# Adding each head's relu to the sum by a DMA, with the half-step lists laid out anew: a two-layer graph kernel on one core

## The chip, the cores and the metric

The kernel runs on one core of one Trainium2 chip. The metric is the device time of one execution in microseconds, median of several runs; lower is better. The engines are named as the profile names them: PE (TensorE, matmuls; PEld is its weight load), DVE (VectorE), ACT (ScalarE), POOL (GpSimd) and SP (SyncE, which issues most DMAs). POOL can issue DMAs too, and an adding DMA (`accum_op=ALU.add`), which adds what it reads to what stands at its destination, is issued there.

## The reference

There are 16 images (graphs) with N = 1024 nodes of D = 128 features, and an adjacency matrix of 0 and 1 for each image.

```
# layer 0: attention over the graph, with three gates
h  = x @ Ww.T + Wb
e  = (h @ A) @ h.T ;  e = e + e.T
s  = where(adj > 0, e, 0)
att = softmax(s, axis=1) * adj
hp = relu(att @ h)
ic, fc, oc = sigmoid(hp @ wi_u + x @ wi_x), sigmoid(... wf ...), sigmoid(... wo ...)
x  = layernorm(x + oc * tanh(ic * hp + fc * x))
# layer 1: four heads
for each head:  h = x @ conv_w + conv_b
                sc = (h @ attn_w) @ h.T
                hh = relu(tanh(adj * sc) @ h)
x  = layernorm(x + relu(relu(mean of hh over the heads) + x))
```

## The kernel before

**Images and steps.** The main loop runs over the 16 images. In the turn of image b, PE computes layer 1 of image b, while pieces of layer 0 of image b+1 (and the first ones of image b+2) and the end of layer 1 of image b-1 are strewn in between. A turn has 32 steps: step = head * 8 + m. Each step has two half steps (q = 0, 1), so a turn has 64 of them. They are called slots here, 0 to 63.

**The lists.** Which piece runs in which slot is written out by hand, in three lists of 64 strings: `FIRST` for image 0, `PLAN` for images 1 to 14, `LAST` for image 15. `slot(n)` goes through the names of string n and emits their instructions. Each engine works its instructions in the order in which they are emitted, so a list decides every engine's order. The names:

- `d5`, `m5`: `differ` and `differ_more` of pair 5 (below). If the pair's scores come later in the turn than the slot, the pair of the previous image is meant (`m15`, and `d14`, `d15` at the end for this image).
- `e`: the next piece of `layer1_end` of the previous image: first the DVE transpose of the sum of heads (`turn_sums`, L335), which goes by way of DRAM to `y`; then two elementwise operations (L1040, L1042) that read `y`, a layernorm in parts, and the DMA to the output (L1046, issued on POOL).
- `r`, `j`, `u`: weights of layer 1. `rows` are projections, `join_rows` four small POOL operations on `hx` and `h` for a group of one head (L796 to L799), `head_uT` a PE projection that ACT copies (L283).
- Capital letters and the rest: pieces of layer 0 of the next image, such as `S` (scores, read by ACT), `T` (transposes), `E` (edges, L475 on POOL), `A` (mask and exponentials), `B` (weighing and the matmuls of the attention), `H` and `h` (the projection `h` and its bias, L411 on DVE), `Q` (projection of q), `G`, `R` (second half of the attention), `P Y F f i o I O V N D` (gates, tanh, layernorm, transposes). With a `+` ahead the piece belongs to the image after the next.

**Pairs.** In layer 1 a head has eight blocks of 128 rows, taken two by two, block i and block i + 4. Such a pair (class `Pair`, number 4 * head + i, so 16 per image) takes two steps, four slots. In each slot PE computes 128 x 512 scores (tag `sc`, three PSUM buffers), DVE multiplies them with the adjacency (L829, L831), and after two slots ACT takes the tanh (L836). The second product, tanh times h, is done with seven products instead of eight, as in Strassen's way: `differ` is a DVE addition (L840), `differ_more` a DVE addition and an adding DMA of 256 KB on POOL's queue (L891, L892). The early products (`early`, numbers 1, 2, 3) of pair p run in slots 4p+4 and 4p+5, the late ones (`late`, numbers 4 to 7) in slots 4p+10 and 4p+11; the late ones read what the adding DMA wrote.

**The end of a head.** After its last pair the products are put together: `keep_early` on ACT, `combine` on DVE (L924 to L929), `sum_up` (L936 on POOL, then the relu on ACT, L940 for head 0, straight into the sum, or L942 for the others) and half a step later `sum_end`, which adds the relu `w` (128 x 1024) to `sum_t` (L948, on POOL). For heads 1 and 2 this falls into the same turn, for head 3 into the next one: `sum_up` after slot 8, `sum_end` after the even slot 10 and ahead of the odd slot 11. There `turn_sums` can begin. In image 15, head 3 is done in another way (`last_step`, `last_back`), and `ready_last` transposes the sum of heads 0 to 2 on PE (L1000), right after the last `sum_end`. So `sum_end` adds 3 x 16 - 1 = 47 times.

**Other order.** `land()` in each step issues the waiting second halves of transposes through DRAM on SP. `w` has one buffer, pairs have three.

Of the kernel before, what the change touches and what calls it, by code (L numbers as in the profile page):

```python
# [15 lines left out]
ALU = mybir.AluOpType  # L16
# [3 lines left out]
P = 128  # L20
# [4 lines left out]
def two_layer_adjacency_kernel(  # L25
# [19 lines left out]
    nc = tc.nc  # L45
    B, N, D = x.shape
# [761 lines left out]
    acc1_t, sum_t, kept, hx_t = {}, {}, [], {}  # L808
# [4 lines left out]
    class Pair:  # L813
# [130 lines left out]
        def sum_end(self):  # L944
            if self.i < BH - 1 or self.hd == 0:
                return
            w = acc1_t[self.b, self.hd, 1][:, :4].rearrange("p k n -> p (k n)")
            nc.gpsimd.tensor_add(sum_t[self.b], sum_t[self.b], w)  # L948

    def last_step(b, m):  # L950
        hd = H - 1
# [171 lines left out]
    for g in range(2):  # L1123
# [2 lines left out]


    PLAN = [
        "B3", "E4 L5 T5 m15", "", "j0.0 A4 L6", "", "d0", "E5 T6 m0", "E6 r2 r3 B4",
        "d1 L7 r6 A5 r7", "m1", "B5 j0.1", "A6 d2", "+W E7", "", "u1.0 e", "+Q0 u1.1 m2 B6 A7",  # L1130
        "B7 j1.1 j1.0", "d3", "+L0 m3 e X R0 e", "+E0 G0 G1 G2 e e e G3 G4 G5",
        "G6 G7 e +L1 R1 d4", "P e m4", "", "", "", "+L2", "+E1 d5", "m5 d6 u2.0 e", "+H0 Y +h0",
        "+Q1 m6 F +S0", "+T0", "+H1 u2.1 +A0 +h1 j2.0", "d7 +S1 f i +T1", "", "m7", "o d8 +S2",
        "j2.1", "+S3 u3.0 +T2 m8 I0", "I1", "", "", "d9 O0 +S4", "m9 O1", "Va", "Vb u3.1",
        "+E2 d10", "+S5 m10 Vc", "+T3", "Vd N0 d11 j3.0", "+H2 m11", "+h2 +B0 +L3", "D",
        "d12 +S6", "m12 +T4", "j3.1", "+S7", "d13", "m13 +A1", "", "+E3", "+B1 u0.0",
        "+A2 u0.1 +A3", "+L4", "d14 r5 r0 m14 r4 +B2 d15 r1",
    ]

    FIRST = [  # L1140
        "S5 A0", "m15", "E1 B0", "u1.0", "L3 A1", "S6 d0 E2", "A2 S7 B1 u1.1 m0",
        "L4 B2 T3 T4 L5", "d1 E3", "E4 A3 j1.0 m1", "E5", "T5 B3 d2", "+W A4 L6", "E6", "B4 L7",
        "+Q0 m2 T6 A5", "", "E7 A6 B5 u2.0 d3 u2.1", "+L0 m3 B6 j1.1", "+E0 A7", "+L1 B7 d4",
        "m4", "R0", "", "G0", "+L2 G1 G2", "+E1 G3 G4 d5", "G5 m5 G6 d6 G7", "j2.0 R1 P +H0 +h0",
        "+Q1 m6 +S0 X", "+T0", "+H1 +A0 +h1", "d7 +S1 +T1", "Y", "m7 j2.1", "F d8 +S2", "",
        "+S3 f +T2 m8 i", "", "o", "I0 u3.0 I1", "d9 +S4", "O0 m9 O1", "u3.1", "Va Vb", "+E2 d10",
        "+S5 m10 Vc", "Vd +T3 j3.0", "N0 d11", "+H2 m11", "+h2 +B0 +L3", "D", "d12 +S6",
        "j3.1 m12 +T4", "", "+S7", "d13", "m13 +A1", "", "+E3", "+B1 u0.0", "u0.1 +A2 +A3", "+L4",
        "d14 r0 r5 m14 +B2 d15 r4 r1",
    ]  # L1150

    LAST = [
        "", "m15", "", "j0.0", "", "d0 m0", "", "r7", "r3", "d1", "u1.0 r2 r6 m1", "j0.1 d2", "e",
        "u1.1 j1.1", "m2", "d3", "", "m3", "j1.0", "", "d4", "u2.0 m4", "", "d5", "", "m5 j2.0",
        "", "e", "", "u2.1 d6", "m6", "", "d7", "", "j2.1 m7", "u3.0", "d8", "m8", "", "", "",
        "d9", "m9", "u3.1", "e", "j3.1 d10", "m10", "", "d11 j3.0", "", "m11", "e", "", "e", "e",
        "", "e", "e", "", "e", "", "", "", "",
    ]
    begun.append(True)
    spare.clear()  # L1160
# [2 lines left out]
    for b in range(B):  # L1163
# [37 lines left out]
        for step in range(H * NB):  # L1201
            hd, m = divmod(step, NB)
            i, half = divmod(m, 2)
# [95 lines left out]
```

## Time and profile before

| | |
|---|---|
| median of 3 runs | 2328.73 us (2328.29 to 2329.71) |
| the profiled execution: own time | 2329.8 us |
| the profiled execution: span | 2328.0 us, granted TensorE clock 0.998 |
| from one image's first score matmul to the next, images 1 to 13 | 142.5 to 143.1 us |
| DMA traffic | 327.27 MB, mean 141 GB/s |
| adding DMAs pair<-pair | 252 of 256.0 KB, median 3.7 us from issue to landing |
| out_dram<-y, on the same queue | 15 of 512.0 KB, median 4.7 us |

The profile shows one execution. "Busy" counts an engine's working time; its share is of the span. In a group, "busy, mean ns" are followed by "idle before, releaser": how long the engine stood idle just ahead of these instructions, and what ended most of that. In a list of waits, "L86 <- DVE h L411" is read as: PE, at line 86, waited for what DVE wrote at line 411. Image 0 begins at 63.4 us, image 1 at 210.3, image 2 at 352.8, image 14 at 2064.8 and image 15 at 2200.6.

### The profile page before, as it was taken

Reading aid. Unit: us, or ns where it says so; the run is one execution under the profiler, and the core shown is the slowest. Engines: PE = TensorE matmul, PEld = TensorE weight load, DVE = VectorE, ACT = ScalarE, POOL = GpSimd, SP = SyncE. Lnnn points to the kernel's source line nnn. Section 1 sums busy time; section 2 is a strip of 40 time slices with the busy share of each in tenths; the row PEclk is TensorE's granted clock in tenths of the full one; section 3 lists DMA queues with packets and bytes.
Section 4 is the critical chain, followed back from the end, with each engine's and each line's share of the span. In section 5 each row is a group of like instructions: output and inputs, shape, how many; then the busy total and the mean of one; then the engine's idle time right before and its main releaser. Section 6 shows DMA issues by size and latency. Waiting matters only on the chain. (4 is left out here: it accounts for less than half of the span.)

```text
span 2328.0 us, 40444 instructions
## 1 busy us (share of the span) xinstructions
PE 2304.9 (99%) x14693; PEld 1074.7 (46%) x14693; DVE 2039.5 (88%) x3689; ACT 1292.4 (56%) x2186; POOL 1308.2 (56%) x1129
## 2 busy tenths in 40 slices
PE   9999999999999999999999999999999999999998
PEld 5345544444444444444444444444444444444444
DVE  7879898998989889898898988889898898988777
ACT  6545564555556555555555555556556555554444
POOL 2645656556565655656466564665645646555342
PEclk9999999999999999999999999999999999999999
DMA  4647565575655656556565565756647565573421
GB/s 146 164 95 199 124 144 154 114 195 133 170 133 111 190 137 173 132 123 173 134 180 129 129 179 114 184 133 135 171 105 201 130 165 135 106 184 86 123 55 37
DMA packets 498090, 327.27 MB, mean 141 GB/s; under 512 B 391139, under 2 KB 416482, under 8 KB 497891
## 3 DMA queue, kind: packets, MB, share of 16 engines
q1 hardware_dynamic: 459149, 250.68, 38.8%
q0 software_dynamic: 38448, 73.94, 18.1%
q8 instruction: 116, 1.90, 0.3%
q14 instruction: 83, 0.68, 0.1%
q10 hardware_dynamic: 294, 0.07, 0.0%
HBM read 199.04 MB, written 59.51 MB: 111 GB/s over the span
## 5 line engine op out<-in xcount | busy, mean ns | idle before, releaser
L86 PE MATMUL sc<-uT,x1T 128*64 128x512 f32 x4096 | 1054.4, 593 | 4.0 <-ACT uT L283 1.9
L836 ACT ACTIVATE pair<-pair 128x1024 f32<-128x1024 f32 x504 | 533.3, 1058 | 588.9 <-DVE pair L829 278.7
L892 POOL DMA_DIRECT2D pair<-pair x252 | 225.5, 895 | 723.3 <-ACT pair L836 158.2
L831 DVE TENSOR_TENSOR pair<-sc,adj 128x512 f32<-128x512 f32 x504 | 339.1, 682 | 105.1 <-PE sc L86 103.7
L86 PEld LDWEIGHTS sc<-uT,x1T 128*64 128x64 f32 x4096 | 294.1, 137 | 293.8 <-issue 156.8
L829 DVE SCALAR_TENSOR_TENSOR pair<-sc,adj 128x512 f32<-128x512 f32 x504 | 343.0, 684 | 86.0 <-PE sc L86 81.5
L475 POOL TENSOR_SCALAR edge<-ring 128x1024 uint8<-128x1024 f32 x120 | 361.0, 3010 | 25.2 <-DMA ring<-in_adjT_dram 23.4
L840 DVE TENSOR_TENSOR pair<-pair 128x1024 f32<-128x1024 f32 x252 | 328.8, 1305 | 10.6 <-ACT pair L836 10.6
L864 PE MATMUL late<-pair,h 128*64 128x256 f32 x2016 | 304.8, 380 | 3.7 <-DMA pair<-pair 3.6
L864 PE MATMUL early<-pair,h 128*64 128x256 f32 x2016 | 304.1, 379 | 1.3 <-ACT pair L836 1.3
L864 PE MATMUL late<-pair,hx 128*64 128x256 f32 x2016 | 304.1, 380 | 0.0
L864 PEld LDWEIGHTS early<-pair,h 128*64 128x64 f32 x2016 | 145.3, 137 | 289.7 <-issue 255.2
L86 PE MATMUL acc<-R,h 128*64 128x512 f32 x960 | 232.2, 592 | 1.3 <-ACT h L524 1.3
L864 PEld LDWEIGHTS late<-pair,h 128*64 128x64 f32 x2016 | 145.6, 137 | 185.4 <-issue 129.5
L864 PEld LDWEIGHTS late<-pair,hx 128*64 128x64 f32 x2016 | 146.6, 137 | 178.3 <-issue 142.7
L891 DVE TENSOR_TENSOR pair<-pair 128x512 f32<-128x512 f32 x252 | 187.8, 745 | 3.2 <-PE early L864 2.6
L504 ACT ACTIVATE R<-R,nmax 128x1024 f32<-128x1024 f32 x126 | 144.7, 1148 | 62.8 <-DVE nmax L500 56.4
L492 DVE CUSTOM_DVE_ANT_0 R<-R,edge 128x1024 f32<-128x1024 f32 x120 | 172.8, 1440 | 3.3 <-POOL edge L475 3.0
L527 DVE TENSOR_TENSOR R<-R,ring 128x1024 f32<-128x1024 f32 x120 | 161.6, 1347 | 0.0
L864 PE MATMUL early<-pair,hx 128*64 128x256 f32 x1008 | 152.0, 379 | 0.0
L620 POOL TENSOR_TENSOR x1T<-hp,wu_b 128x1024 f32<-128x1024 f32 x45 | 111.7, 2482 | 69.5 <-DVE hws L626 63.3
L936 POOL TENSOR_TENSOR w<-w 128x512 f32<-128x512 f32 x63 | 84.8, 1346 | 96.5 <-DVE w L926 96.3
(214 smaller groups left out, 2831.2 us busy)
## 6 DMA issues: line engine op xcount, KB each, us to landing
adj<-in_adjT_dram SPq DMA_DIRECT2D x128, 512.0 KB, 4.2
pair<-pair POOLq DMA_DIRECT2D x252, 256.0 KB, 3.7
ring<-in_adjT_dram SPq DMA_DIRECT2D x120, 512.0 KB, 5.0
xT<-in_xT_dram SPq DMA_DIRECT2D x16, 512.0 KB, 7.2
x<-in_x_dram SPq DMA_DIRECT2D x16, 512.0 KB, 5.2
dram_hp<-turn_hp SPq DMA_DIRECT2D x15, 512.0 KB, 2.6
hp<-dram_hp SPq DMA_DIRECT2D x60, 128.0 KB, 3.1
dram_x<-turn_x SPq DMA_DIRECT2D x15, 512.0 KB
```

The costliest lines, as they stand in the source:

```text
L86: nc.tensor.matmul(out[ts(c, HD)], lhsT[:, ts(c, HD)], rhs, start=start, stop=stop)
L475: engine.tensor_scalar(m, t["adj", j], 0.0, None, ALU.is_gt)
L492: nc.vector.tensor_tensor_reduce(to[:, ks], s[:, ks], t["edge", j][:, ks], 1.0, nmax, ALU.mult, ALU.max, top)
L504: nc.scalar.activation(row(j), row(j), AF.Exp, bias=t["nmax", j], accum_out=t["z", j])
L527: nc.vector.tensor_mul(s[:, ks], s[:, ks], adj[:, ks])
L829: nc.vector.scalar_tensor_tensor(to, psv, -1.0, adj, op0=ALU.mult, op1=ALU.mult)
L831: nc.vector.tensor_mul(to, psv, adj)
L836: nc.scalar.activation(s, s, AF.Tanh)
L840: nc.vector.tensor_add(t[:, X3 : N12 + 1 : N12 - X3, :], t[:, N12 : N12 + 1, :].to_broadcast([P, 2, 512]), t[:, B22 : B11 + 1, :],)
L864: nc.tensor.matmul(out[ts(q, HD)], w, self.t[:, at, ts(q, HN)], start=(i == 0 and p in (1, 3, 5, 4)), stop=(i == BH - 1), skip_group_check ...
L891: nc.vector.tensor_add(t[:, B22], t[:, B22], t[:, N12])
L892: nc.gpsimd.dma_start(t[:, N21], t[:, B22], accum_op=ALU.add)
```

## The change

In `sum_end` the POOL tensor operation becomes an adding DMA from SBUF to SBUF of 128 x 1024 float32 (512 KB), issued on POOL: `sum_t += w`. It stands in the same place of the program. All three lists are laid out anew: the same pieces, in other slots. No other instruction is added or taken away. Of the things the prediction speaks of: in `PLAN` the first `e` goes from slot 14 to 11, L1040's from 18 to 17, `m1` from 9 to 11, `j0.1` from 10 to 11, `+H2` from 49 to 47, `+S6` from 52 to 51.

```diff
--- before.py
+++ after.py
@@ -945,7 +945,7 @@
             if self.i < BH - 1 or self.hd == 0:
                 return
             w = acc1_t[self.b, self.hd, 1][:, :4].rearrange("p k n -> p (k n)")
-            nc.gpsimd.tensor_add(sum_t[self.b], sum_t[self.b], w)
+            nc.gpsimd.dma_start(sum_t[self.b], w, accum_op=ALU.add)
 
     def last_step(b, m):
         hd = H - 1
@@ -1126,35 +1126,35 @@
 
 
     PLAN = [
-        "B3", "E4 L5 T5 m15", "", "j0.0 A4 L6", "", "d0", "E5 T6 m0", "E6 r2 r3 B4",
-        "d1 L7 r6 A5 r7", "m1", "B5 j0.1", "A6 d2", "+W E7", "", "u1.0 e", "+Q0 u1.1 m2 B6 A7",
-        "B7 j1.1 j1.0", "d3", "+L0 m3 e X R0 e", "+E0 G0 G1 G2 e e e G3 G4 G5",
-        "G6 G7 e +L1 R1 d4", "P e m4", "", "", "", "+L2", "+E1 d5", "m5 d6 u2.0 e", "+H0 Y +h0",
-        "+Q1 m6 F +S0", "+T0", "+H1 u2.1 +A0 +h1 j2.0", "d7 +S1 f i +T1", "", "m7", "o d8 +S2",
-        "j2.1", "+S3 u3.0 +T2 m8 I0", "I1", "", "", "d9 O0 +S4", "m9 O1", "Va", "Vb u3.1",
-        "+E2 d10", "+S5 m10 Vc", "+T3", "Vd N0 d11 j3.0", "+H2 m11", "+h2 +B0 +L3", "D",
-        "d12 +S6", "m12 +T4", "j3.1", "+S7", "d13", "m13 +A1", "", "+E3", "+B1 u0.0",
-        "+A2 u0.1 +A3", "+L4", "d14 r5 r0 m14 r4 +B2 d15 r1",
+        "u1.0", "B3 E4 m15 A4", "", "j0.0", "L6 E5 B4", "A5 d0", "u1.1 m0", "T6 r7",
+        "L7 r2 +W E6", "A6 r3 d1", "B5 r6", "m1 B6 j0.1 e E7", "", "+Q0 d2 m2", "", "A7", "B7",
+        "e", "d3 R0 m3 e", "e +L0 e j1.0 G0 G1", "G2 G3 G4 G5 e X j1.1", "e G6 G7 R1 d4 +Q1 e P",
+        "m4", "+E0 u2.0", "d5", "m5", "", "d6 e +L1", "+H0 Y j2.0", "+h0 +S0 F f m6", "",
+        "+H1 u2.1 +T0 +h1 d7", "+S1 +A0 i", "+T1", "+S2 m7 +T2", "o", "", "d8", "j2.1 m8", "+S3",
+        "u3.0 I0", "I1 d9 u3.1", "m9", "O0 O1 Va", "Vb +S4", "d10", "m10 Vc +S5 Vd",
+        "+H2 +T3 +L2", "N0 +h2 j3.0", "d11", "m11 j3.1", "D +S6", "d12", "+S7 m12 +T4 +B0", "",
+        "+L3 +E1", "d13", "m13", "+E2", "+A1", "u0.0 +E3", "+B1 u0.1 +L4 +A2", "",
+        "r4 r1 r0 d14 m14 r5 d15 +B2 +A3 +T5 +L5",
     ]
 
     FIRST = [
-        "S5 A0", "m15", "E1 B0", "u1.0", "L3 A1", "S6 d0 E2", "A2 S7 B1 u1.1 m0",
-        "L4 B2 T3 T4 L5", "d1 E3", "E4 A3 j1.0 m1", "E5", "T5 B3 d2", "+W A4 L6", "E6", "B4 L7",
-        "+Q0 m2 T6 A5", "", "E7 A6 B5 u2.0 d3 u2.1", "+L0 m3 B6 j1.1", "+E0 A7", "+L1 B7 d4",
-        "m4", "R0", "", "G0", "+L2 G1 G2", "+E1 G3 G4 d5", "G5 m5 G6 d6 G7", "j2.0 R1 P +H0 +h0",
-        "+Q1 m6 +S0 X", "+T0", "+H1 +A0 +h1", "d7 +S1 +T1", "Y", "m7 j2.1", "F d8 +S2", "",
-        "+S3 f +T2 m8 i", "", "o", "I0 u3.0 I1", "d9 +S4", "O0 m9 O1", "u3.1", "Va Vb", "+E2 d10",
-        "+S5 m10 Vc", "Vd +T3 j3.0", "N0 d11", "+H2 m11", "+h2 +B0 +L3", "D", "d12 +S6",
-        "j3.1 m12 +T4", "", "+S7", "d13", "m13 +A1", "", "+E3", "+B1 u0.0", "u0.1 +A2 +A3", "+L4",
-        "d14 r0 r5 m14 +B2 d15 r4 r1",
+        "S5 A0", "m15", "E1", "B0", "E2", "L3 u1.0 A1 d0", "S6 u1.1 A2 B1 m0", "E3 L4 S7 T3 B2",
+        "L5 +W", "T4 d1", "E4 A3", "m1", "B3 T5 L6", "+Q0 d2 E5 A4 m2", "", "B4", "A5", "j1.0 T6",
+        "E6 d3 u2.0 A6 m3 L7 B5", "+L0 E7 u2.1", "B6", "A7 d4 +Q1", "B7 m4", "+E0", "R0 d5",
+        "G0 G1 m5 G2", "G3 G4 j1.1", "d6 G5 G6 G7 j2.1 +L1", "+H0 R1 P", "+h0 +S0 m6", "",
+        "+H1 +T0 X +h1 d7", "+S1 +A0", "+T1 Y", "+S2 m7 F +T2", "j2.0", "f", "d8", "m8 i", "+S3",
+        "o", "d9", "m9", "", "I0 +S4", "I1 u3.0 d10", "O0 m10 u3.1 O1 +S5 Va", "+H2 +T3 +L2 Vb",
+        "j3.1 j3.0 +h2", "d11", "m11 Vc", "Vd +S6", "N0 d12", "+S7 m12 +T4 D +B0", "", "+L3 +E1",
+        "d13", "m13", "+E2", "+A1", "+E3", "+B1 u0.0 +L4 u0.1 +A2", "",
+        "d14 r0 r5 r1 r4 m14 d15 +B2 +A3 +T5 +L5",
     ]
 
     LAST = [
-        "", "m15", "", "j0.0", "", "d0 m0", "", "r7", "r3", "d1", "u1.0 r2 r6 m1", "j0.1 d2", "e",
-        "u1.1 j1.1", "m2", "d3", "", "m3", "j1.0", "", "d4", "u2.0 m4", "", "d5", "", "m5 j2.0",
-        "", "e", "", "u2.1 d6", "m6", "", "d7", "", "j2.1 m7", "u3.0", "d8", "m8", "", "", "",
-        "d9", "m9", "u3.1", "e", "j3.1 d10", "m10", "", "d11 j3.0", "", "m11", "e", "", "e", "e",
-        "", "e", "e", "", "e", "", "", "", "",
+        "", "m15", "", "j0.0", "d0", "m0", "u1.0", "", "d1 r6 r7", "u1.1 r3 m1", "r2 j0.1", "d2",
+        "", "", "m2", "j1.0", "e", "d3 m3", "", "d4", "", "j1.1 m4", "", "", "d5 u2.0", "",
+        "m5 j2.0", "d6", "u2.1", "", "m6", "e", "", "d7", "m7 u3.0", "", "j2.1", "d8 m8", "", "",
+        "", "u3.1 d9 m9", "e", "", "d10 e", "j3.0 j3.1", "m10 e", "e", "d11", "", "", "m11 e e",
+        "", "", "", "e", "", "", "", "", "", "", "", "",
     ]
     begun.append(True)
     spare.clear()
```

## Prediction

> **What bounds the kernel now.** I read the busy table first, then the groups by form of the lines the change touches, then TensorE's waits, whole and by stretches, then the timeline where a wait stood. Busy table and groups:
>
> ```profile
> PE 2304.9 (99%) x14693; PEld 1074.7 (46%) x14693; DVE 2039.5 (88%) x3689; ACT 1292.4 (56%) x2186; POOL 1308.2 (56%) x1129
> L948 POOL TENSOR_TENSOR sum<-sum,w 128x1024 f32<-128x1024 f32 x47 | 128.8, 2740 | 4.5 <-ACT w L942 4.5
> L335 DVE STREAM_TRANSPOSE turn_sum<-sum 128x1024 f32<-128x1024 f32 x15 | 18.7, 1245 | 4.1 <-POOL sum L948 3.9
> L1046 POOL DMA_DIRECT2D out_dram<-y x15 | 17.0, 1134 | 0.9 <-ACT y L260 0.9
> ```
>
> TensorE is the bound, GpSimd is 56% busy, and the add that goes costs 128.8 us of an engine with time to spare. One reader of its result waits, DVE's transpose of the sum: 3.9 us in the run. In the timeline, starts of successive matmuls lie 0.215 us apart for 512 columns and 0.107 for 256; over all matmuls this spacing adds up to 2283.0 us, so 45.0 of the 2328.0 is not issue. Set against the clock, 18.8 of it has gone by 190 us (some 14 before 110), 11.2 go between 190 and 2131 us (0.7 to 0.8 per image of 142.6 us), 6.9 in 2131 to 2214, 8 behind. That is all the lists can win. TensorE's waits, whole span:
>
> ```profile
> PE late L864 <- DMA pair<-pair: 3.6, 4, 1.2
> PE sc L86 <- DVE h L411: 3.1, 12, 0.8
> PE sc L86 <- ACT uT L283: 1.9, 2, 1.2
> PE sc L86 <- DVE pair L831: 1.8, 2, 1.1
> PE early L864 <- ACT pair L836: 1.3, 3, 0.8
> ```
>
> Columns: us in all, times, longest. Only the second comes once per image; the others are in image 0 and in image 14 (2064 to 2200 us). Windows of image 0, a steady image and image 14 (us, busy of PE, PEld, DVE, ACT, POOL, granted clock, DMA share, GB/s):
>
> ```profile
> 63.00:111.00 48.00, 44.61 (x262) 18.44 (x260) 43.74 (x73) 28.33 (x50) 32.90 (x26) 1.00 0.73 169
> 159.00:168.00 9.00, 7.12 (x36) 2.86 (x34) 8.57 (x26) 4.49 (x8) 0.41 (x2) 0.81 0.25 39
> 582.00:630.00 48.00, 48.00 (x328) 23.06 (x326) 45.90 (x93) 26.36 (x44) 25.57 (x22) 1.00 0.62 131
> 2134.00:2182.00 48.00, 44.20 (x288) 19.65 (x286) 43.65 (x89) 24.47 (x44) 25.44 (x29) 1.00 0.30 62
> ```
>
> PE is short by 3.4, 1.9, 0 and 3.8 us; DVE is nearly full in each. The second window in the timeline:
>
> ```profile
> 160.81 1.08 PE L86 MATMUL sc<-xT,qT 128*64 128x512 f32 x4 [0.71 <-DVE pair L831]
> 163.06 1.55 PE L86 MATMUL sc<-uT,x1T 128*64 128x512 f32 x4 [1.17 <-ACT uT L283]
> ```
>
> Two stalls follow one another, and the granted clock of 0.81 adds about 1.6 us by the spacing of the next matmuls.
>
> **The add itself.** GpSimd loses 47 x 2.74 = 128.8 us and gains 47 issues; the nearest issue of this size (L1046, 512 KB) takes 1.13, so 53 us. On the path this is worth nothing, since no wait of TensorE ends on L948 but the one at the end. It could help DVE beside it: L840's add takes 1.21 us alone and 1.28 beside L948 in the timeline, and all DVE work beside L948 is stretched by some 6 us in the run, nearly all of it hidden. The Trainium skill (SBUF — State Buffer, Who interferes with whom) says that a DVE operation with two SBUF inputs contends with a GpSimd operation that reads SBUF, over a shared port pair held exclusively. By that rule up to the whole 128.8 us of L948 could come back to DVE; the trace shows a stretch of 0.07 us on an add, so the row decides, and I take 0.
>
> The sum is ready later. The adding DMAs of this trace are pair<-pair, 256 KB, 2.4 to 6.7 us from the end of issue, median 2.8. Their queue, q0, has 18.1% of 16 engines' time, over 252 of them some 1.5 us each. So 512 KB is about 1.1 + 2.4 + 1.5 = 5.0 us; the bounds are 3.4 (an issue and the shortest landing) and 13 (twice the longest). I take 5.0, since plain 512 KB transfers to HBM on this queue took 4.6 to 6.0. The fit in the Trainium skill (DMA: Bandwidth & Descriptors, Anatomy of one DMA) makes it an estimate of 2.0 + 1.2 = 3.2 us, which would leave nobody waiting; but it makes 256 KB 2.6, and the profile has 3.7.
>
> Who waits: turn_sum moves from slot 14 to 11 (a slot is 2.2 us), but the step j0.1, four GpSimd operations of 3.8 us together, no longer stands ahead of the sum, nor does m1. The relu is ready 21.8 us into an image (L936 at slots 7 to 8, then L942); issue to 22.9, landing about 27; by DVE's running sum turn_sum's turn is at 28.9. So no wait; at 13 us it would be 6, and all of DVE's work stands behind it. From turn_sum to the first use of y (L1040) the trace has 10.3 us; that use moves to slot 17 and would wait some 1.5 us on DVE. Three score buffers and the long products after it cover this. w is written again seven slots later, so its release costs nothing.
>
> **The queue.** m1's pair DMA now stands 4.5 to 5 us behind the sum's on GpSimd's queue. It is issued at about 27.5, lands at 30.8 to 31.4 undisturbed, and is needed at 32.7 by the late product: 1.3 to 1.9 us to spare. Before, the tightest pairs have 0.8 to 1.5 (medians by pair), and they do not stall. One landing in ten takes 4.8 or more instead of 2.8, and would use up the margin. I take 0.1 us an image, +1.4; bounds 0 and +14 (1.0 in each of 14 images, as the pair waits before were 0.9 each).
>
> **The new lists.** I summed DVE's rows against TensorE's slots with the old lists, where the lag agrees with the trace to about 0.9 us, and then with the new.
> - Image 0, late part: DVE's lag in slots 40 to 48 falls from 1.1 to 3.3 to at most 1.0; the two stalls (0.76, 1.34 in spacing) and the low clock (1.6) go: -3.7. Slots 54 to 58 rise to 2.7, where the trace's steady images reach 2.3 without a stall: +0.4. Together -3.3; bounds -3.7 and -2.5.
> - Image 0, early part: lag falls from at most 3.2 to 1.9 in slots 8 to 16. The pair DMA waits (1.9 in this window) may go; the ACT one (1.3) is not touched. -1.5; bounds -3 and 0.
> - Image 14: slots 30 to 43 fall from 1.8 to 0.5, slots 44 to 47 rise to 1.9. Of 6.9, the pair L831 and L829 waits (2.1) mostly go, ACT uT and the pair DMA perhaps: -1.7; bounds -3.5 and +1.
> - Steady images: +H2 moves from slot 49 to 47 and its reader, +S6, from 52 to 51: one slot more between. The h wait (3.1 in 12) needs 0.25 on average: -2.5; bounds -3.1 and 0. DVE's maximal lag goes from 1.4 to 1.7: nothing.
>
> **The tail.** Here the sum is on the path:
>
> ```profile
> 2305.39 2.37 POOL L948 TENSOR_TENSOR sum<-sum,w 128x1024 f32<-128x1024 f32 x1 [2.32 <-ACT w L942]
> 2308.09 1.09 PE L1000 MATMUL pt_base<-ident,sum 128*128 128x128 f32 x8
> ```
>
> TensorE's turn comes at 2307.3 and it waits 0.8. With the DMA the sum is there at about 2310.2 (a tail with little other traffic, so a bit below 5.0 after 2305.39), and everything behind shifts: +2.2; bounds +0.5 and +4.
>
> **Sum.** -3.3 + 0 (add) - 1.5 - 1.7 - 2.5 + 1.4 + 2.2 = -5.4. The profiled execution was 2329.8 for a span of 2328.0; -5.4 on its span is 2322.6, its time 2324.4. It stood 1.1 above the median of the runs, so the median goes from 2328.73 to 2323.3.
>
> **Rivals.**
> - *The queue decides (slower).* The sum's DMA takes more than about 9.5 us from issue; then m1's transfer, on the same queue, passes its 32.7 in every image and turn_sum holds DVE. For: 256 KB took up to 6.7 after issue, and DMA share rises by 47 x 3 us / 2328 = 6%. Against: steady pairs meet no such thing now, with 0.62 DMA share. Price 0.8 to 1.0 in each of 14 images in place of the queue's 1.4: +11.2 to +14, with the other terms, -6.8, +4.4 to +7.2; with 0.3 an image of turn_sum's wait handed on to TensorE 4 more. That is 2333 to 2340. The Trainium skill (DMA: Bandwidth & Descriptors, SWDGE vs HWDGE vs iDMA) has accumulating transfers only on GpSimd's path, with one queue allocated; it speaks against the change, and the trace shows q0 as the only software queue.
> - *The stalls stay (same).* Image 0 and 14 hang on what the lists hardly touch: ACT's h and uT, the pair DMA. Then only the clock term and half of the h wait are won: -1.6 - 1.3 + 0.4 + 1.4 + 2.2 = +1.1, so 2329.8, within 2326 and 2332.
> - *The lists make new waits (slower).* If my lag sum is off by its 0.9 us where slots 54 to 58 and 44 to 47 rose, the stalls only move within images 0 and 14, and in steady images the L1040 wait reaches TensorE with 0.3 to 0.5 each, 4.2 to 7 in all. With -2.5 + 1.4 + 2.2 beside it that is +5.3 to +8.1: 2334 to 2337.
>
> **How the numbers follow.** Forecast 0.42, stalls stay 0.28, queue 0.22, new waits 0.08. A measurement of this kernel tells about 0.2% (4.7 us) from no change, so faster means below 2324.1, slower above 2333.4: 0.42, 0.28 and 0.30. The best ends of all terms give -12.8 (2316), the worst +16.5 (2345). With some 0.06 left out below and 0.1 above, the range is 2317 to 2338; the likeliest case's own is 2317 to 2324.
>
> **What would show it.** Right: a landing of the sum's DMA near 5 us after issue; no wait of turn_sum on it beyond 0.5; no 0.81 clock in 159 to 168; the h L411 wait gone from TensorE's list; pt_base waiting about 3 us on a DMA. Wrong: pair<-pair waits at slot 14 in most images, a period above 142.9, a wait at L1040 that TensorE shares, or the DVE pair waits still in image 14.

## The result and the profile after

The changed kernel takes 2392.14 us (median of 4 runs, 2390.91 to 2393.45) against 2328.51 us (2327.13 to 2329.71): a ratio of 1.027, with a 95% interval of 1.0258 to 1.0282. The forecast was 2323.3, within 2317 and 2338. The profiled execution took 2391.07 us, its span is 2389.2.

The page's busy table and the line of the adding DMAs' queue, the group of `differ`'s addition, then TensorE's waits over the whole span (us in all, times, longest):

```profile
PE 2325.0 (97%) x14693; PEld 1066.0 (45%) x14693; DVE 2048.8 (86%) x3689; ACT 1289.7 (54%) x2186; POOL 1149.4 (48%) x1129
q0 software_dynamic: 45216, 98.59, 23.0%
L840 DVE TENSOR_TENSOR pair<-pair 128x1024 f32<-128x1024 f32 x252 | 384.8, 1527 | 25.6 <-ACT pair L836 25.0
```

```profile
PE sc L86 <- DVE pair L831: 35.3, 13, 3.1
PE late L864 <- DMA pair<-pair: 7.9, 6, 2.3
PE sc L86 <- DVE pair L829: 2.6, 1, 2.6
PE early L864 <- ACT pair L836: 2.4, 3, 1.3
PE pt_base L1000 <- DMA sum<-w: 2.2, 1, 2.2
```

GpSimd lost 159 us of busy time: the 47 additions (128.8 us) are gone, their 47 issues take 51.0 us, and most of the rest is that the small `hx` operations L796 and L798 took 63 us less. TensorE gained nothing by it. TensorE has a new wait, 13 times, 2.7 us each: for DVE's product of scores and adjacency (L831). The wait for `h` (L411), 3.1 us before, is gone. The 252 additions L840 are the same instructions as before, but they took 384.8 us instead of 328.8.

By images, from the starts of the first score matmuls: image 0 takes 146.8 us in both kernels; images 1 to 13 take 146.7 instead of 142.6, which is 53 us together; image 14 takes 140.2 instead of 135.8, image 15 and the end 131.3 instead of 127.4. So 53 of the 61 us of span lie in images 1 to 13, and there they are one event, repeated once per image. Here it is in the timeline of one image (start and duration in us; the idle time before it in brackets, and what ended it):

```profile
1003.97 3.10 DVE L840 TENSOR_TENSOR pair<-pair 128x1024 f32<-128x1024 f32 x1
1004.40 1.58 POOL L936 TENSOR_TENSOR w<-w 128x512 f32<-128x512 f32 x1
1010.53 2.53 POOL L620 TENSOR_TENSOR x1T<-hp,wu_b 128x1024 f32<-128x1024 f32 x1
1010.74 3.83 DVE L840 TENSOR_TENSOR pair<-pair 128x1024 f32<-128x1024 f32 x1 [1.27 <-ACT pair L836]
1014.49 1.27 DVE L831 TENSOR_TENSOR pair<-sc,adj 128x512 f32<-128x512 f32 x2
1015.22 3.50 PE L86 MATMUL sc<-xT,qT 128*64 128x512 f32 x8 [2.67 <-DVE pair L831]
```

L840 takes 1.22 us undisturbed (the median of the 252). The one of `d5` took 3.10: GpSimd's L936 began 0.43 us after it, and L840 ended 1.09 us after L936 had. The one of `d6` took 3.83, beside the product L620 and the two `hx` operations behind it. Together DVE lost 1.9 + 2.6 us within 11 us. L831 behind them came late, no score buffer was free, and TensorE stood for 2.67 us. Then the granted clock fell. It is the third window here; the first two are of image 0 and are read further below (columns as in the prediction):

```profile
159.00:168.00 9.00, 9.00 (x62) 4.30 (x60) 8.92 (x19) 6.28 (x10) 1.79 (x2) 1.00 0.42 76
181.00:190.00 9.00, 6.68 (x38) 3.00 (x36) 7.37 (x12) 5.78 (x12) 3.77 (x2) 0.81 0.79 210
1014.00:1020.00 6.00, 4.78 (x18) 1.70 (x20) 3.91 (x9) 2.53 (x4) 4.16 (x5) 0.72 0.00 0
```

In the third window it is 0.72: the records of the clock have 0.5 for 3.41 of its 6 us, from 1014.99 on, and by the spacing of the matmuls this adds 1.6 us. So an image loses 2.7 + 1.6, less the 0.25 of the `h` wait: the 4.1 that its period shows.

### The profile page after: what moved, and what is told of

Its sections match the earlier page's. It is cut to its first block, busy times and chain, and to the rows that moved or that the text cites. A ratio compares the mean times of both kernels' runs of the same rounds, so it can differ in the third digit from the quotient of the medians.

```text
span 2389.2 us, 40597 instructions
## 1 busy us (share of the span) xinstructions
PE 2325.0 (97%) x14693; PEld 1066.0 (45%) x14693; DVE 2048.8 (86%) x3689; ACT 1289.7 (54%) x2186; POOL 1149.4 (48%) x1129
## 5 line engine op out<-in xcount | busy, mean ns | idle before, releaser
L831 DVE TENSOR_TENSOR pair<-sc,adj 128x512 f32<-128x512 f32 x504 | 337.2, 678 | 98.1 <-PE sc L86 96.7
L840 DVE TENSOR_TENSOR pair<-pair 128x1024 f32<-128x1024 f32 x252 | 384.8, 1527 | 25.6 <-ACT pair L836 25.0
L829 DVE SCALAR_TENSOR_TENSOR pair<-sc,adj 128x512 f32<-128x512 f32 x504 | 338.5, 681 | 66.6 <-PE sc L86 64.4
L475 POOL TENSOR_SCALAR edge<-ring 128x1024 uint8<-128x1024 f32 x120 | 357.1, 2979 | 72.6 <-DMA ring<-in_adjT_dram 59.0
L864 PEld LDWEIGHTS late<-pair,h 128*64 128x64 f32 x2016 | 143.9, 137 | 191.3 <-issue 133.0
L864 PEld LDWEIGHTS late<-pair,hx 128*64 128x64 f32 x2016 | 144.8, 137 | 180.3 <-issue 143.5
L86 PE MATMUL sc<-xT,qT 128*64 128x512 f32 (+3 forms) x684 | 149.2, 548 | 35.3 <-DVE pair L831 35.3
L891 DVE TENSOR_TENSOR pair<-pair 128x512 f32<-128x512 f32 x252 | 179.4, 712 | 3.1 <-PE early L864 0.3
L492 DVE CUSTOM_DVE_ANT_0 R<-R,edge 128x1024 f32<-128x1024 f32 x120 | 165.9, 1382 | 1.6 <-POOL edge L475 1.3
L620 POOL TENSOR_TENSOR x1T<-hp,wu_b 128x1024 f32<-128x1024 f32 x45 | 110.0, 2444 | 105.8 <-DVE hws L626 99.0
L527 DVE TENSOR_TENSOR R<-R,ring 128x1024 f32<-128x1024 f32 x120 | 152.2, 1269 | 0.0
```

The costliest lines, as they stand in the source:

```text
L86: nc.tensor.matmul(out[ts(c, HD)], lhsT[:, ts(c, HD)], rhs, start=start, stop=stop)
L475: engine.tensor_scalar(m, t["adj", j], 0.0, None, ALU.is_gt)
L492: nc.vector.tensor_tensor_reduce(to[:, ks], s[:, ks], t["edge", j][:, ks], 1.0, nmax, ALU.mult, ALU.max, top)
L527: nc.vector.tensor_mul(s[:, ks], s[:, ks], adj[:, ks])
L829: nc.vector.scalar_tensor_tensor(to, psv, -1.0, adj, op0=ALU.mult, op1=ALU.mult)
L831: nc.vector.tensor_mul(to, psv, adj)
```

## The experiments

Theory P: DVE work with two inputs in SBUF is held up while a GpSimd operation reads SBUF, and the new lists bring such pairs together at a place where DVE has no slack. The rivals were the adding DMA itself, and lists that are too dense for DVE without any contention. Each ratio is to runs of the kernel before on the same chip.

**Lists and DMA apart.** Old lists with the adding DMA:

```diff
-            nc.gpsimd.tensor_add(sum_t[self.b], sum_t[self.b], w)
+            nc.gpsimd.dma_start(sum_t[self.b], w, accum_op=ALU.add)
```

> Theory P (port): in the new lists DVE's two-input additions fall beside GpSimd tensor operations and are held up; the lists cost the time, not the adding DMA. Then the old lists with the adding DMA lack the 4.2 us an image; only the tail's 2.2 us stay, and turn_sum waits some 2 us on DVE in each image for the later sum: 2329 to 2335. Theory Q (the DMA: its transfer, its issue or its queue slow DVE or the pair DMAs): about 2385 to 2392 with the old lists too. Theory W (the new lists and the DMA only hurt together): 2328 to 2333, as P, but then the next run is fast as well.

And the reverse, the new lists with the tensor operation:

> New lists, the sum added by GpSimd's tensor operation as before. P: the time stays, less the tail's 2.4 us: 2387 to 2392, with the 2.7 us wait of sc<-xT,qT on DVE in every image. Q: about 2328 to 2333. W: about 2328 to 2333.

| | tensor operation | adding DMA |
|---|---|---|
| old lists | 1 (2329.3 us) | 1.0063 (1.0048 to 1.0078), 2343.7 us |
| new lists | 1.048 (1.0463 to 1.0498), 2442.9 us | 1.027 (1.0258 to 1.0282), 2392.1 us |

Both were missed in size. The lists are what costs, but the DMA is not neutral: it costs 0.6% with the old lists, where DVE lost little beside GpSimd's addition, and it gains 2% with the new ones. There the tensor operation meets DVE work of two SBUF inputs (new lists with the tensor operation, timeline):

```profile
1062.01 5.05 DVE L675 SCALAR_TENSOR_TENSOR u<-u,gate,x 128x128 f32<-128x128 f32 x8
1062.41 2.65 POOL L948 TENSOR_TENSOR sum<-sum,w 128x1024 f32<-128x1024 f32 x1
```

The eight small operations lose 2.9 us to L948. Against the median of each kind of operation, DVE's work beside L948 is 89 us longer in that run, 40 of it on L675.

**Which pairs.** In slot 28 of `PLAN` GpSimd's order is turned round:

```diff
-"+H0 Y j2.0"
+"+H0 j2.0 Y"
```

> After, but in slot 28 of PLAN the four small GpSimd operations of j2.0 stand ahead of the large one of Y (L620); nothing else moves. P: the L840 beside them falls from 3.83 us to about 1.3, the 2.7 us wait of TensorE in each image and the lower granted clock behind it go: 2330 to 2345. Theory D (the new lists just put too much DVE work too close, no contention): L840 beside L620 is not the cause and the time stays at 2388 to 2393.

Measured 2394.48, ratio 1.0279 (1.0264 to 1.0295): no gain, as theory D had it. But the profile doesn't speak for D. L840 did fall to 1.53 us and the wait at `sc<-xT,qT` to 0.4; a new wait of 2.06 came 8 us later, since L620 was now late for its reader (DVE waited 1.95) and held up another operation:

```profile
1018.17 2.36 POOL L620 TENSOR_TENSOR x1T<-hp,wu_b 128x1024 f32<-128x1024 f32 x1 [1.28 <-DVE hws L626]
1018.57 1.99 DVE L633 TENSOR_SCALAR gate<-gate 128x8 f32<-128x8 f32 x1 [0.28 <-ACT gate L632]
```

L633 works on eight elements per partition and takes 0.2 us alone. It reads one tensor, in SBUF, so what is held up is not only work with two inputs; which other operations are was not tried.

The other pair, L936 in the middle of `d5`'s addition, came about because the edge piece L475 stood ahead of L936 on GpSimd. It goes back to slot 19:

```diff
-"e +L0 e j1.0 G0 G1" ... "+E0 u2.0"
+"e +L0 +E0 e j1.0 G0 G1" ... "u2.0"
```

> After, but the edge piece +E0 (L475) goes from slot 23 back to slot 19 of PLAN, so that L936 no longer starts in the middle of the L840 of d5 (3.1 us). P: that L840 falls to 1.5 to 2.1 us, DVE reaches the stall 1 to 1.9 us earlier, so TensorE's wait falls from 2.7 to 0.8 to 1.7 us; the one beside L620 stays: 2362 to 2385. D: 2388 to 2393.

Measured 2362.39, 1.014 (1.0125 to 1.0155), at the lower edge of P's range. That L840 fell to 1.47; TensorE's wait for L831 and one window of it:

```profile
PE sc L86 <- DVE pair L831: 13.3, 10, 1.8
```

```profile
1004.00:1010.00 6.00, 4.99 (x32) 2.14 (x32) 5.31 (x9) 2.31 (x4) 4.09 (x5) 1.00 0.03 10
```

TensorE waited 1.0 us there, and the clock stays at 1.00: of the 2.0 us won per image (146.7 to 144.7), the larger part is the 1.6 of the lower clock.

With that edit, `m5` too goes back where the old list has it, so that its DMA holds L620 back until `d6`'s addition is over:

> The run with +E0 in slot 19, and also m5 moved from slot 25 to 27, where the old list has it. GpSimd's L620 stands behind m5's DMA, so it should start after the L840 of d6 and not in the middle of it. P (two-input DVE work held up beside GpSimd, where DVE has no slack): L840 at d6 falls from 3.0 to 3.8 us to 1.2 to 1.5, the rest of TensorE's wait for L831 goes: 2332 to 2348. D (the block only moves to the next DVE operation beside L620, as when hx was put ahead): 2355 to 2368.

Measured 2368.27, 1.0163 (1.0148 to 1.0178): a miss for P's number. L840 took 1.23, but the hold-up had moved, as the second case of the expectation had it: the next addition of the kind met the next L620:

```profile
1005.67 2.37 POOL L620 TENSOR_TENSOR x1T<-hp,wu_b 128x1024 f32<-128x1024 f32 x1
1005.90 2.69 DVE L891 TENSOR_TENSOR pair<-pair 128x512 f32<-128x512 f32 x1
```

L891 takes 0.68 alone. With the last sum of image 15 as a tensor operation on top:

> The run with +E0 in slot 19 and m5 in slot 27, and for image 15's head 2 alone the tensor operation in place of the adding DMA. The wait of pt_base falls from 2.2 to 0.8 us or less; 1.5 to 4 us less than that run, under either theory.

Measured 2363.45, 1.0139 (1.0122 to 1.0156): 4.8 less in the medians, a little more than was expected.

**Taking the reading away.** Moving things had only moved the collision. So `Y`'s product was left out of the changed kernel, and GpSimd wrote zeros to the same tile; the gate fc is then not computed as in the reference:

```diff
+            if g == 1:
+                nc.gpsimd.memset(t["hw"], 0.0)
+                return
             nc.gpsimd.tensor_mul(
```

> After, but the product of Y (weigh_hp(1), L620, for the gate fc) is left out: GpSimd writes zeros of the same 128x1024 with a memset, which reads nothing from SBUF. P: the L840 of d6 falls from 3.83 us to 1.2 to 1.6 although GpSimd writes beside it, TensorE's wait for L831 falls from 2.7 to below 0.9 us and the lower granted clock goes: 2332 to 2355. If any GpSimd operation beside L840 held it up (writes too), or if the lists put too much DVE work there anyway: 2380 to 2393.

Measured 2354.65, 1.0103 (1.0088 to 1.0118); L843 is L840 here:

```profile
996.23 1.14 POOL L621 MEMSET x1T<- 128x1024 f32 x1
996.46 1.35 DVE L843 TENSOR_TENSOR pair<-pair 128x1024 f32<-128x1024 f32 x1 [1.27 <-ACT pair L839]
998.46 1.08 PE L86 MATMUL sc<-xT,qT 128*64 128x512 f32 x4 [0.18 <-DVE pair L834]
```

GpSimd writes for 0.9 us beside the addition, and this loses 0.13. (The zeros also take GpSimd 1.14 us instead of 2.5, so this run frees it a little besides.) With `+E0` in slot 19 as well:

> Both causes taken from after's steady images: the product of Y (L620 for the gate fc) left out and set to zero by a memset, and +E0 in slot 19. P: the two hold-ups (1.9 and 2.6 us of DVE in each image) are all that the new lists lose there; with both gone TensorE waits for DVE's pair less than 0.2 us an image, the image takes 142.4 to 142.9 us, and only the tail's 4 us and the pair DMA waits stay: 2334 to 2345. If something else in the new lists costs time too: 2348 to 2355, as with the first edit alone.

Measured 2342.58, 1.0053 (1.0039 to 1.0066), a time as expected; an image takes 142.8 to 143.9 us, a little more than expected. With both hold-ups gone, 50 of the 63 us are gone.

**Putting one in.** The kernel before, with one name moved by one slot:

```diff
-"+E1 d5", "m5 d6 u2.0 e"
+"+E1 d5 m5", "d6 u2.0 e"
```

> The kernel before, only m5 in slot 26 instead of 27, ahead of d6. GpSimd then reaches the large L620 sooner, as in the new list, and d6's L840 (1.22 us, just ahead of L620 in before) should meet it. P: L840 at d6 takes 2.5 to 3.8 us in most images, TensorE waits for DVE's pair up to 1.5 us an image: 2333 to 2355. If DVE has slack enough in the old list, or L620 still comes behind: 2327 to 2331.

Measured 2362.64, 1.014 (1.0126 to 1.0154). `d6`'s addition ended 0.6 us ahead of L620 in the kernel before:

```profile
987.54 1.23 DVE L840 TENSOR_TENSOR pair<-pair 128x1024 f32<-128x1024 f32 x1 [0.53 <-ACT pair L836]
989.36 2.60 POOL L620 TENSOR_TENSOR x1T<-hp,wu_b 128x1024 f32<-128x1024 f32 x1
```

With `m5` moved it meets it:

```profile
996.90 4.29 DVE L840 TENSOR_TENSOR pair<-pair 128x1024 f32<-128x1024 f32 x1 [1.12 <-ACT pair L836]
997.52 2.58 POOL L620 TENSOR_TENSOR x1T<-hp,wu_b 128x1024 f32<-128x1024 f32 x1
1001.11 0.68 DVE L831 TENSOR_TENSOR pair<-sc,adj 128x512 f32<-128x512 f32 x1
1001.84 1.08 PE L86 MATMUL pT_q<-xT,q_w 128*64 128x512 f32 x4 [2.13 <-DVE pair L831]
```

The time lies above P's range, since L840 lost 3.1 us and not up to 2.6, and TensorE waited 2.1 in 11 images and not up to 1.5. What P says of the cause holds, and it is shown from both sides: what is taken out gives the time back, and one slot in the old list costs 33 us. Counting overlaps of more than 0.3 us over the traces of ten of these kernels: L829 and L831, which read one input from PSUM, lie beside L620 486 times and never lose more than 0.04 us. L840 loses 2.5 us beside L620 (median of 76), L891 0.7 (of 91).

**What the DMA costs in the old lists.** In the first of the runs above TensorE waits 8.3 us in 13 times for a pair's adding DMA, mostly pair 14's at the start of an image, and 2.1 at the end. Head 2 alone goes back to the tensor operation:

```diff
+            if self.hd == 2:
+                nc.gpsimd.tensor_add(sum_t[self.b], sum_t[self.b], w)
+            else:
+                nc.gpsimd.dma_start(sum_t[self.b], w, accum_op=ALU.add)
```

> Old lists, the adding DMA for heads 1 and 3 alone, head 2 (and so the last sum of image 15) by GpSimd's tensor operation. Theory K (queue): with the DMA for all heads, the pair DMAs at the end of an image stand behind head 2's sum on the same queue and make TensorE wait at the start of the next image (0.3 to 1.2 us, 11 images), and the tail waits 2.4 us and then runs at a lower clock for 1.6: here both go, 2330 to 2335. Theory L (the load of all the adding transfers, wherever they stand): two thirds of the 14.4 us stay but for the tail's 4: 2335 to 2338.

Measured 2332.44, 1.0012 (1.0003 to 1.0022), beside a before of 2330.17: head 2's transfers make 12 of the 14 us, some 4.5 of them in image 15 and the end (132.3 us with all sums by DMA, 127.8 here). But it isn't the queue: head 2's transfer lands some 7 us before the image's end, and pair 14's is issued 1.8 us before it. The second try was SP's order:

```diff
-"d12 +S6", "m12 +T4"
+"d12 +S6 +T4", "m12"
```

> Old lists, adding DMA for all heads, and the transpose +T4 one slot earlier (52 instead of 53). Theory M (crowding through SP): head 2's sum, 512 KB, moves beside the four second halves of +T4's transpose; these land later, SP issues the adjacency loads behind them 1 to 2 us later, and these meet pair 14's adding DMA at the image's end, which lands in 5.9 us instead of 4.6 and makes TensorE wait. With +T4 earlier the loads go out earlier: pair 14 lands in 4.5 to 5.3, the waits at the start of the images fall below 0.2: 2334 to 2339. Theory K (the one software queue): the sum's DMA has landed 4 us before pair 14's is issued in any case; nothing changes, 2342 to 2346.

Measured 2343.96, 1.006 (1.0046 to 1.0074): theory M fails. The loads did go out 3 to 4 us earlier, and pair 14 still landed after a median of 6.2 us from the end of its issue, while the sum itself landed 3 us ahead of the image's end and not 7. What is left of these theories is the load of the DMA engines. The last 3 us of an image and the first 3 of the next, in the kernel before and then in old lists with the DMA (the last two columns are the DMA share and GB/s):

```profile
1062.70:1065.70 3.00, 3.00 (x18) 1.00 (x16) 2.90 (x4) 1.81 (x4) 1.80 (x2) 1.00 0.94 338
1065.70:1068.70 3.00, 3.00 (x20) 1.14 (x18) 1.89 (x3) 0.99 (x2) 2.52 (x1) 1.00 0.95 238
```

```profile
1065.00:1068.00 3.00, 3.00 (x18) 1.00 (x16) 2.92 (x4) 1.83 (x4) 0.92 (x1) 1.00 1.04 415
1068.00:1071.00 3.00, 3.00 (x20) 1.14 (x18) 1.88 (x3) 0.99 (x2) 2.42 (x1) 1.00 1.04 312
```

The stretch is nearly full already, and another 512 KB pushes what follows later: over the last 15 us of images 1 to 12 the mean share is 0.92 before, 1.03 with the DMA and 0.92 again with head 2 back on the tensor operation. That taking the transfer away helps is shown; that the fullness is the way is read off these windows and was not tried by itself.

**The one part that should win.** The kernel before with `+H2` and `+h2` two slots earlier, as in the new lists:

> The kernel before, only +H2 in slot 47 instead of 49 and +h2 in 48 instead of 50, as in the new list: the one part of the new lists that should win something. Expected: the wait of sc<-xT,qT for h (L411), 3.1 us in all, goes, and its image's 0.25 us with it: 2325 to 2328 beside a before of 2328 to 2330. If DVE's or TensorE's order there is worse for it: 2330 to 2340.

Measured 2329.95, 0.9999 (0.999 to 1.0008). The wait stayed, at 2.7 us in 11 times: these two names alone don't make it go, and what in the new list does was not tried. No version tried beats the kernel before.

## Why the prediction was wrong

- **The step that failed** is the one that weighed contention and let a single row decide: "the trace shows a stretch of 0.07 us on an add, so the row decides, and I take 0". That row was L948 beside L840 where they overlapped in the kernel before, 12 times all in the same position:

```profile
950.01 1.28 DVE L840 TENSOR_TENSOR pair<-pair 128x1024 f32<-128x1024 f32 x1
950.17 3.37 POOL L948 TENSOR_TENSOR sum<-sum,w 128x1024 f32<-128x1024 f32 x1
```

L840 kept its time, but L948 took 3.4 us instead of its shortest 2.37: GpSimd was the one that lost, where it had time to spare. Other rows of the same trace had DVE losing. Beside L948 itself L527 took 1.87 us (median of 14) instead of 1.2, so that DVE's work beside it is 13 us longer by the medians and not some 6. L891 took 1.34 us (median) beside L620 instead of 0.68, L492 2.50 instead of 1.22, and of the three L840 beside L620 one took 2.31. The page on SBUF in the Trainium skill (SBUF — State Buffer, Who interferes with whom) had it: two SBUF inputs on DVE against a reading GpSimd operation, full block, while an operation that only writes doesn't contend. The runs agree: 3.83 us beside the product, 1.35 beside the memset.
- **Its consequence** was in the new lists: "DVE's maximal lag goes from 1.4 to 1.7: nothing". The sum took DVE's rows at their durations in the old places. In the new places two additions are 4.5 us longer in every image, and TensorE waits 2.7 and loses 1.6 to the clock. This term was 0 in the sum and measured +53 in images 1 to 13, with the `h` wait's gain already taken off.
- **The steady `h` wait** (-2.5) went, worth 3.1 us; that two names moved by two slots are enough for it was wrong.
- **Image 0** (-3.3 and -1.5): the stalls at 160 and 163 us and the low clock in 159 to 168 went, as said. But pair DMA landed after 6.9 us in a stretch with adjacency loads at 210 GB/s; TensorE waited 2.3 us at 185.0 and the clock was 0.81 there. Nothing was won. The 1.6 us of low clock at 163 also belonged to the one execution: in the traces of five other kernels with the old `FIRST` list the same two stalls leave the clock at 1.00, and image 0 takes 144.6 to 146.2 us. **Image 14** (-1.7) lost 4.4: TensorE waited 2.6 us for DVE's L829 and 1.5 and 1.6 for pair DMAs, the last while a sum's DMA took 10.5 us.
- **The sum's DMA** was sized well: the 47 issues take 51.0 us (53 taken), median 5.5 us to landing (5.0 taken), `turn_sum` never waited for it, pair 1 was not late. Its engine time is (23.0% of 2389.2 - 18.1% of 2328.0) / 47 = 2.7 us of 16 engines each.
- **The tail** (+2.2) measured +3.9. `pt_base` waited 2.2; before, the matmuls' own spacing leaves 0.1, since the 0.8 of the prediction is the weight load's wait. The last matmul came 2.4 us later in its image. The other 1.5 lie behind all the work and were in no term: GpSimd's last DRAIN takes 5.45 us instead of 3.94.
- **The queue** as a rival (slower) didn't come true: `m1`'s transfer was not late. That its price, 11 to 14 us, is close to the 14 us of the old lists with the DMA is chance; there pair 14 is late after head 2's sum has landed. **New waits from the lists** was the case that came true; it had 0.08 and a price of 0.3 to 0.5 an image, since it was made from an error of the lag and not from contention.

## What to carry to other kernels

When a list or schedule moves work of two engines against each other, a duration taken from the old places is no price for the new ones. Price each operation beside each neighbour it will have, from all rows where the trace has such a pair, and take the worst pair where the engine has no slack. Look at both partners' durations in such a row: one that kept its time may have kept it at the other's cost. What a freed engine is worth depends on what its work stood beside: the same replacement cost 0.6% with one list and gained 2% with the other.

## What was not expected of the hardware

- **Who loses is not settled by who starts,** as far as the profile's starts tell (its spans on GpSimd are rough). In the last list edit L840 began 0.62 us before L620 and lost 3.07 us; at 141 us in the kernel before, L840 began 0.11 us before L620 and kept its 1.22, while L620 took 3.34 instead of 2.4. Within one trace, that of the run with `+E0` moved, L840 began 0.3 us before L620 both at 567.2 us, where it lost nothing, and at 1869.5, where it lost 2.55.
- **The granted clock goes by stretches of 3.41 us.** In each trace the slow records (0.5) last 3.41 us or twice that, but for the one that runs into the end, and their starts lie whole multiples of 3.413 us apart. With the fourteen traces divided into these stretches (the first 70 us, the last 25 and stretches already slow left out), add up TensorE's idle time in each: all 53 with 2.0 us or more were followed by a slow one, and none with less than 1.86; between, 3 of 12 were. So a wait's length alone doesn't tell: one of 2.68 us that lay across two stretches kept the full clock (at 284.4 us, new lists with the tensor operation), one of 1.96 lost it (at 2226.1 us, old lists with `m5` moved). There the images that lost it take about 1.3 us more (146.1 instead of 144.8). In the changed kernel the slow stretches of images 1 to 13 lie 146.77 us apart, 43 times 3.413, and its period is 146.7; whether the one sets the other was not tried.
- **DMAs issued on GpSimd lengthen its last DRAIN.** It takes 3.94 us in the kernel before (267 such DMAs), 4.55 with 31 more (heads 1 and 3), 5.37 with 46 more and 5.45 with 47 more; with the new lists and the tensor operation it is 3.94 again.
